# Summing the last expert layer into the output with TensorE instead of VectorE

## The chip, the cores and the metric

The kernel runs on one core of one Trainium2 chip. The metric is device time in microseconds (us), the median of several runs. A core has five engines, each with an instruction queue of its own: TensorE (PE; its weight loads are shown apart as PEld), VectorE (DVE), ScalarE (ACT), GpSimd (POOL) and SyncE (SP). SP, ACT and POOL also issue DMA transfers. The engines wait for each other through semaphores. PE reads two operands from SBUF, a stationary one that is loaded as weights and a moving one that is streamed, and writes into PSUM, where a row of matmuls can add up.

## The reference, cut to what matters

The program is four layers over an image tensor of 2 x 256 x 32 x 32. Only its last lines bear on the change: the residual sum of the mixture-of-experts layer, and the way back from tokens to an image.

```python
    logits = jnp.einsum('bsd,de->bse', x, gate_w) + gate_b
    probs = jax.nn.softmax(logits, axis=-1)
    top_probs, top_idx = jax.lax.top_k(probs, 2)
    top_probs = top_probs / jnp.sum(top_probs, axis=-1, keepdims=True)
    ...
    return jnp.einsum('bseo,bse->bso', expert_out, dispatch)
...
    t = t + _L3_ffn_ref(_ln_t(t), L3_ffn_gate_w, L3_ffn_gate_b, L3_ffn_w1, L3_ffn_w2, L3_ffn_w3)
    x = _from_tokens(t, x)      # t.transpose(0, 2, 1), then to 2 x 256 x 32 x 32
```

So for each of 2048 tokens, the output is t plus w0 times the row of its first expert plus w1 times the row of its second expert, and channels, not tokens, come first in the output.

## The kernel before, in words

Tokens lie 128 to a tile: t is an SBUF tensor of 128 x 16 x 256 (`NT` = 16 tiles of 256 channels, `C`). Four tiles (`TPC`) make a chunk of 512 tokens (`TC`); two chunks make an image (`NB` = 2). Channels are two halves of 128 (`NCC`, index cc).

`experts` runs the chosen experts group by group, 128 rows each. Its last step in a group is a copy on DVE (L1576) and an indirect DMA from POOL (L1577), which scatters the 128 result rows into a DRAM tensor `yd` of 4096 x 256: the first experts' rows of all tokens first, then the second experts' rows. How many groups run depends on the data; the last of them stand in nested branches (L1604).

The final stage begins at L1656, after the last branch. For each chunk, `combine` (L1364) loads the expert rows from `yd` with DMAs issued alternately by SP (k = 0) and ACT (k = 1), 24 in all, of one tile (128 KB) or two tiles (256 KB). Then DVE adds each row tile, times its weight column, into t (L1378): two sums to a tile, 32 in all. After that `net.transposed` (L175) turns the four tiles of the chunk on PE, half by half of the channels, into one PSUM bank of 128 x 512 (L179), and ACT copies the bank to the output tile (L1671) in the order of pixels that the image has. After the second chunk of an image, SP stores the two halves of the image (L1675), 512 KB each.

The order on each engine is that of the program: DVE's sums in order of tiles, PE's turnings behind them, ACT's copies behind those, and the row loads of ACT in the same queue as its copies. `make_identity` gives `net.ident`, the 128 x 128 identity in SBUF. `gates[1].weight` is 128 x 2 x 16: a column for each expert choice k and tile.

Of the kernel before, what the change touches and what calls it, by code (L numbers as in the profile page):

```python
# [10 lines left out]
F32 = mybir.dt.float32  # L11
# [5 lines left out]
PSUM = bass.MemoryType.PSUM  # L17
DRAM = bass.MemoryType.DRAM

P = 128  # L20
NB = 2
HW = 1024
W = 32
T = NB * HW
C = 256
NCC = C // P
NT = T // P
TC = 512
NCH = T // TC
TPC = TC // P  # L30
# [1333 lines left out]
def combine(net, gate, t, j, pool, n=TPC):  # L1364

    nc, layer = net.nc, gate.layer
    y = pool.tile([P, 2, TPC, C], F32, tag="yl", name=f"{layer}_yl_{j}")
    for i in range(0, TPC, n):
        for k, eng in enumerate((nc.sync, nc.scalar)):
            at = k * T + j * TC + i * P  # L1370
            eng.dma_start(
                y[:, k, i : i + n],
                gate.yd[at : at + n * P, :].rearrange("(i p) c -> p i c", p=P),
            )
    for i in range(TPC):
        ti = j * TPC + i
        for k in range(2):
            nc.vector.scalar_tensor_tensor(  # L1378
                t[:, ti, :], y[:, k, i, :], gate.weight[:, k, ti : ti + 1], t[:, ti, :],
                ALU.mult, ALU.add,  # L1380
            )
        if i % n == n - 1:
            yield
# [228 lines left out]
@with_exitstack  # L1612
def conv_attn_hybrid(ctx: ExitStack, tc: tile.TileContext, a: dict, out: bass.AP):
    nc = tc.nc
    net = Net(ctx, tc, a["cols"], a["rows"])
    main = ctx.enter_context(tc.tile_pool(name="main", bufs=1))
    x = main.tile([P, NCC, NB, HW], F32, name="x")
    lg = Taps.logits(main.tile([P, 40 * W], F32, tag="lg", name="lg0"))
    conv_dram = ctx.enter_context(tc.tile_pool(name="conv_dram", bufs=1, space=DRAM))
    with tc.tile_pool(name="conv_w", bufs=2) as convw:  # L1620
        def load_x(b):
            for cc in range(NCC):
                nc.sync.dma_start(x[:, cc, b, :], a["x"][b, cc])

        load_x(0)
        taps = Taps(net, convw, main, x, a["l1_w1"], a["l1_w2"])
        layer0(
            net, x, a["x"],
            [a[f"m1_{k}"] for k in ("in_w", "out_w", "xproj_w", "dt_w")],
            [a[f"m2_{k}"] for k in ("in_w", "out_w", "xproj_w", "dt_w")],  # L1630
            lambda: load_x(1), taps, conv_dram, lg,
        )
    tokens = ctx.enter_context(tc.tile_pool(name="tokens", bufs=1))
    t = tokens.tile([P, NT, C], F32, name="t")
    with (
        tc.tile_pool(name="counters", bufs=1) as counters,
        tc.tile_pool(name="gate", bufs=2) as gpool,
        tc.tile_pool(name="gate_dram", bufs=1, space=DRAM) as gdram,
    ):
        with ExitStack() as first:  # L1640
            weigh = layer1(first, net, x, t, taps, lg)
            net.counters(counters)
            gates = [Gate(net, n, t, a[f"{n}_gate_w"], gpool, gdram) for n in ("l2", "l3")]
            linear_attention(
                net, t, weigh, gates[0].chunk,
                *[a[f"l2_{k}"] for k in ("wq", "wkv", "wm", "w1", "w2")]
            )
        with tc.tile_pool(name="scores", bufs=1) as spool:
            scores = Scores(net, spool, a["l3_wqkv"])
            experts(net, "l2", gates[0], a["l2_experts"], scores.make)  # L1650
            softmax_attention(
                net, t, lambda *a: combine(net, gates[0], t, *a), gates[1].chunk,
                scores,
            )
        experts(net, "l3", gates[1], a["l3_experts"])
        with (  # L1656
            tc.tile_pool(name="f_sb", bufs=2) as sb,
            tc.tile_pool(name="f_y", bufs=4) as ypool,
            tc.tile_pool(name="f_ps", bufs=4, space=PSUM) as ps_f,
        ):  # L1660

            for b in range(NB):
                o = [sb.tile([P, HW], F32, tag=f"o{cc}", name=f"out_{b}_{cc}") for cc in range(NCC)]
                for a in range(2):
                    for _ in combine(net, gates[1], t, 2 * b + a, ypool, 1 if b == a else 2):
                        pass
                    for cc in range(NCC):
                        tiles = [t[:, (2 * b + a) * TPC + i, :] for i in range(TPC)]
                        ps = net.transposed(ps_f, tiles, cc, "mm")
                        to = o[cc].rearrange("p (r a h c) -> p a r c h", a=2, h=W // 2, c=2)  # L1670
                        nc.scalar.copy(  # L1671
                            to[:, a], ps.rearrange("p (r c h) -> p r c h", c=2, h=W // 2)
                        )
                        if a:
                            nc.sync.dma_start(out[b, cc], o[cc])  # L1675

# [73 lines left out]
```

## Time and profile before

| what | value |
|---|---|
| median of 3 runs | 2173.26 us (2171.8 to 2174.47) |
| the profiled execution's own time | 2172.59 us |
| its span, first to last instruction | 2170.9 us |
| granted PE clock over the span | 0.913 of full speed |
| PE busy over the span | 1889.3 us (87%) |
| DVE busy over the span | 1402.7 us (65%) |
| last scatter of expert rows landed | at 2146.80 us |
| DVE's 32 sums (L1378) of the final stage | from 2150.04 to 2164.5 us |
| ACT's last copy (L1671) ends | at 2166.15 us |

Times within the span count from its start. A row of the timeline or of the chain of waits begins with its start and its length in us; then come the engine, the line of the kernel, the operation, the tiles it writes and reads, and a count if rows were merged. In square brackets stands how long the engine had been idle before it and on what it waited. "x4: 272/278/2010" in an answer on one line gives the shortest, the median and the longest of four instructions in ns. Lines of matmuls overlap, since PE is pipelined.

### The profile page before, as it was taken

The page shows a single profiled execution, that of the slowest core. Times are in us where ns is not written, and L with a number is a line of the kernel's source. Part 1 is how long each engine was busy: PE and PEld are TensorE (multiplying, and loading weights), DVE is VectorE, ACT ScalarE, POOL GpSimd, SP SyncE. Part 2 cuts the span into 40 slices and gives each one's busy share as a digit, 9 for nine tenths or more (in the row PEclk, how much of TensorE's full clock was granted, in tenths as well). Part 3 has the DMA queues.
Part 4 walks back from the last instruction along what each step waited for, and adds up shares of the span by engine and source line. Part 5 has one row for each costly group of instructions (what it writes and reads, how often), then busy time and mean ns, then how long its engine had stood idle before and what let it go on. Part 6 is the DMA issues. An engine that isn't in the chain of part 4 may idle for free.

```text
span 2170.9 us, 27318 instructions
## 1 busy us (share of the span) xinstructions
PE 1889.3 (87%) x9652; PEld 1345.8 (62%) x9652; DVE 1402.7 (65%) x2210; ACT 959.9 (44%) x1611; POOL 1027.6 (47%) x726
## 2 busy tenths in 40 slices
PE   6888798888989879799989989949999699859996
PEld 2364555556555645455656556539999467649995
DVE  6999997999999999897405575652222544442223
ACT  4676776767777767653213454411010132301111
POOL 3796887959698695964225420012332000023331
PEclk8969988897989889899999999969999799979997
DMA  2121121111212111310030100028999200059998
GB/s 107 45 69 40 40 67 35 53 40 45 63 48 60 35 48 34 86 40 20 5 64 1 49 15 10 20 86 304 323 332 333 83 10 10 20 208 320 334 330 294
DMA packets 90499, 223.87 MB, mean 103 GB/s; under 512 B 35467, under 2 KB 51728, under 8 KB 79732
## 3 DMA queue, kind: packets, MB, share of 16 engines
q1 hardware_dynamic: 77636, 198.29, 27.2%
q0 software_dynamic: 7728, 19.15, 3.0%
q10 hardware_dynamic: 4992, 4.59, 0.7%
q8 instruction: 81, 1.33, 0.3%
q14 instruction: 62, 0.51, 0.1%
HBM read 204.60 MB, written 19.37 MB: 103 GB/s over the span
## 4 chain that ended last, share of the span: by engine, by line
PE 32%; DVE 22%; issue 19%; POOL 12%; ACT 9%; DMA 5%; POOLq 0%; SPq 0%; ACTq 0%; DVEq 0%
DVE m_h L472 11%; DVE m_ya L449 5%; PE acc L769 3%; POOL x L1527 3%; POOL l_yd L1577 3%; PE m_ht L440 3%; PE av L1283 3%; POOL m_h L461 3%; PE early_acc L769 2%; PE sc L1257 2%; ACT m_da L468 2%; DMA l_yd<-y,target 2%; PE h L1106 2%; PE w L1115 1%; PE m_xd_ps L351 1%
## 5 line engine op out<-in xcount | busy, mean ns | idle before, releaser
L461 POOL TENSOR_TENSOR m_h<-m_du,m_b 128x1024 f32<-128x1024 f32 x254 | 594.4, 2364 | 227.6 <-PE m_ht L440 126.8
L440 PE MATMUL m_ht<-ident,m_h 128*128 128x128 f32 x2048 | 360.2, 306 | 107.2 <-DVE m_ya L449 78.4
L440 PEld LDWEIGHTS m_ht<-ident,m_h 128*128 128x128 f32 x2048 | 266.2, 156 | 299.0 <-issue 105.2
L468 ACT ACTIVATE m_da<-m_delta,m_aneg 128x512 f32<-128x512 f32 x512 | 349.0, 690 | 219.7 <-DVE m_h L472 218.8
L1527 POOL DMA_INDIRECT x<-l_zd,source x82 | 84.5, 1031 | 569.9 <-DVE source L1472 215.3
L449 DVE SCALAR_TENSOR_TENSOR m_ya<-m_ht,m_ct,m_ya 128x512 f32<-128x512 f32 x448 | 319.3, 732 | 29.2 <-PE m_ht L440 27.8
L472 DVE TENSOR_TENSOR_SCAN m_h<-m_da,m_state,m_h 128x512 f32<-128x512 f32 x256 | 316.8, 1268 | 26.9 <-POOL m_h L461 20.7
L472 DVE TENSOR_TENSOR_SCAN m_h<-m_da,m_h 128x512 f32<-128x512 f32 x256 | 302.8, 1208 | 25.3 <-ACT m_da L468 15.2
L1557 PEld LDWEIGHTS h<-xts,we 128*128 128x128 f32 x2528 | 298.3, 194 | 6.8 <-issue 2.9
L1557 PE MATMUL h<-xts,we 128*128 128x128 f32 x2528 | 299.4, 277 | 1.9 <-issue 1.5
L1564 DVE TENSOR_TENSOR hid<-hid,h 128x512 f32<-128x512 f32 x79 | 54.3, 687 | 255.5 <-PE h L1557 252.0
L1563 ACT ACTIVATE hid<-h 128x512 f32<-128x512 f32 x79 | 47.2, 597 | 381.7 <-issue 299.3
L1571 PE MATMUL o<-we,hid 128*128 128x256 f32 x632 | 150.4, 380 | 2.2 <-DVE y L1576 1.6
L1577 POOL DMA_INDIRECT l_yd<-y,target x79 | 79.0, 1000 | 142.7 <-DVE y L1576 136.4
L1571 PEld LDWEIGHTS o<-we,hid 128*128 128x128 f32 x632 | 113.7, 190 | 15.7 <-DVE y L1576 2.8
L336 PE MATMUL m_conv<-m_pre,m_taps 128*128 128x512 f32 x240 | 114.6, 596 | 6.8 <-ACT m_gate L498 5.6
L769 PE MATMUL early_acc<-x,early 128*98 128x448 f32 (+24 forms) x308 | 100.5, 453 | 0.0
L769 PE MATMUL acc<-x,pair 128*98 128x416 f32 (+21 forms) x308 | 94.0, 452 | 0.0
L1576 DVE COPY y<-o 128x256 f32<-128x256 f32 x79 | 33.6, 425 | 69.3 <-PE o L1571 69.3
L309 PE MATMUL m_in<-x,m_in_sb 128*128 128x512 f32 x128 | 67.7, 653 | 7.6 <-ACT m_pre L313 5.2
L769 PEld LDWEIGHTS acc<-x,pair 128*98 128x98 f32 x308 | 47.6, 167 | 39.1 <-issue 33.6
L494 PE MATMUL m_g<-x,m_gate_sb 128*128 128x512 f32 x128 | 66.5, 633 | 3.9 <-ACT m_o L168 2.1
(318 smaller groups left out, 2849.2 us busy)
## 6 DMA issues: line engine op xcount, KB each, us to landing
we<-in_l_experts_dram SPq DMA_DIRECT2D x82, 1536.0 KB
m_b<-m_bd SPq DMA_DIRECT2D x128, 256.0 KB
w<-in_l_w_dram SPq DMA_DIRECT2D x21, 256.0 KB
l_zd<-l_z SPq DMA_DIRECT2D x7, 512.0 KB
l_yl<-l_yd SPq DMA_DIRECT2D x10, 256.0 KB
l_yl<-l_yd ACTq DMA_DIRECT2D x10, 256.0 KB
early<-taps SPq DMA_DIRECT2D x7, 343.0 KB
pair<-taps SPq DMA_DIRECT2D x7, 343.0 KB
```

The costliest lines, as they stand in the source:

```text
L309: nc.tensor.matmul(ps, lhsT=self.in_sb[:, kc, mc * P : (mc + 1) * P], rhs=self.xt[:, kc, tok], start=(kc == 0), stop=(kc == NCC - 1),)
L336: nc.tensor.matmul(ps, lhsT=self.taps[:, dc * 4 + k, :], rhs=pre[:, dc, k : k + TC], start=(k == 0), stop=(k == 3),)
L440: nc.tensor.transpose(ps[:, dc * P : (dc + 1) * P], hs[dc // G][:, dc % G, i * P : (i + 1) * P], net.ident,)
L449: nc.vector.scalar_tensor_tensor(ya[:, i, :], ps, c, ya[:, i, :], ALU.mult, ALU.add)
L461: (nc.vector if start and n == 0 else nc.gpsimd).tensor_mul(h, du[:, g * G : (g + 1) * G, :], b.unsqueeze(1).to_broadcast(half))
L468: nc.scalar.activation(da, delta[:, dc, :], AF.Exp, scale=self.aneg[:, i : i + 1])
L472: nc.vector.tensor_tensor_scan(h, da, h, 0.0 if first else state[:, n, dc : dc + 1], ALU.mult, ALU.add)
L769: nc.tensor.matmul(a[:, lo - 16 * k : hi - 16 * k, co : co + n], lhsT=lhsT, rhs=self.x[:, kc, b, lo - r0 : hi - r0, ci : ci + n], start=(u ...
L1527: nc.gpsimd.indirect_dma_start(out=x, out_offset=None, in_=zd[:, :], in_offset=bass.IndirectOffsetOnAxis(ap=source[:, g : g + 1], axis=0), ...
L1557: nc.tensor.matmul(ps[:, at], lhsT=w12[:, s, kc, at], rhs=xt[:, kc * P : (kc + 1) * P], start=(kc == 0), stop=(kc == NCC - 1),)
L1571: nc.tensor.matmul(ps[:, :C], lhsT=ht[:, mc * P : (mc + 1) * P], rhs=w[:, 8 + mc, :], start=(mc == 0), stop=(mc == NHC - 1),)
L1577: nc.gpsimd.indirect_dma_start(out=yd[g], out_offset=bass.IndirectOffsetOnAxis(ap=target[:, g : g + 1], axis=0), in_=y, in_offset=None, bo ...
```

## The change

DVE no longer sums and PE no longer turns finished sums. Instead PE does both at once: a matmul with a tile of t (or of expert rows) as the stationary operand and a 128 x 128 diagonal matrix as the moving one gives the turned tile, scaled token by token, and PSUM adds up the three terms: t with the identity, the first expert's rows with a diagonal of its weights, the second's with another. There are eight sums of 128 x 512, one to each PSUM bank.

- DVE makes the 32 diagonals `by` first, the identity times a weight column (L1668 of the new kernel).
- The rows are loaded by 16 DMAs of 256 KB, eight from SP and eight from ACT, all issued at the start of the stage, each into a tile of its own (L1675).
- POOL makes `wide`, 128 x 512: zero, with the identity in its first 128 columns. The first matmul into a bank uses it as its moving operand, and so writes all 512 columns.
- PE first turns all of t: 8 matmuls of 512 columns and 24 of 128, then for each chunk the 16 matmuls with expert rows, 64 in all (L1689).
- The eight copies from PSUM to the output tiles are made by DVE, six of them, and by ACT, the two of the second image's second half of channels (L1711, L1713). The four stores stay with SP.

In the built program the first instruction of this stage on each of the five engines waits for all that came before the last branch, the last scatter's landing included; before, DVE's, PE's and ACT's did so only through the loads. Nothing ahead of the stage moves on any engine.

```diff
-            tc.tile_pool(name="f_y", bufs=4) as ypool,
-            tc.tile_pool(name="f_ps", bufs=4, space=PSUM) as ps_f,
+            tc.tile_pool(name="f_y", bufs=1) as ypool,
+            tc.tile_pool(name="f_ps", bufs=1, space=PSUM) as ps_f,
         ):
+            by = ypool.tile([P, 2, NT, P], F32, name="f_by")
+            y = {}
+            ps = {}
+            for i in range(NT):
+                for k in range(2):
+                    nc.vector.tensor_scalar_mul(
+                        by[:, k, i, :], net.ident, gates[1].weight[:, k, i : i + 1]
+                    )
+            for i in range(0, NT, 2):
+                for k, eng in enumerate((nc.sync, nc.scalar)):
+                    at = k * T + i * P
+                    y[i, k] = ypool.tile([P, 2, C], F32, name=f"f_yl_{i}_{k}")
+                    eng.dma_start(
+                        y[i, k], gates[1].yd[at : at + 2 * P, :].rearrange("(i p) c -> p i c", p=P),
+                    )
+            wide = ypool.tile([P, TC], F32, name="f_wide")
+            nc.gpsimd.memset(wide, 0.0)
+            nc.gpsimd.tensor_copy(wide[:, :P], net.ident)
+
+            def turn(i, a, rhs, stop=False):
+                first = rhs is wide
+                at = i % TPC * P
+                for cc in range(NCC):
+                    to = ps[i // TPC, cc]
+                    nc.tensor.matmul(
+                        to if first else to[:, at : at + P], lhsT=a[:, cc * P : (cc + 1) * P],
+                        rhs=rhs, start=first, stop=stop,
+                    )
+
+            for i in range(NT):
+                if i % TPC == 0:
+                    for cc in range(NCC):
+                        ps[i // TPC, cc] = ps_f.tile([P, TC], F32, name=f"f_{i // TPC}_{cc}")
+                turn(i, t[:, i, :], net.ident if i % TPC else wide)
             for b in range(NB):
...
                 for a in range(2):
-                    for _ in combine(net, gates[1], t, 2 * b + a, ypool, 1 if b == a else 2):
-                        pass
+                    j = 2 * b + a
+                    for i in range(j * TPC, (j + 1) * TPC):
+                        for k in range(2):
+                            turn(i, y[i // 2 * 2, k][:, i % 2, :], by[:, k, i, :], stop=(k == 1 and i % TPC == TPC - 1))
                     for cc in range(NCC):
-                        tiles = [t[:, (2 * b + a) * TPC + i, :] for i in range(TPC)]
-                        ps = net.transposed(ps_f, tiles, cc, "mm")
-                        to = o[cc].rearrange("p (r a h c) -> p a r c h", a=2, h=W // 2, c=2)
-                        nc.scalar.copy(
-                            to[:, a], ps.rearrange("p (r c h) -> p r c h", c=2, h=W // 2)
-                        )
+                        to = o[cc].rearrange("p (r a h c) -> p a r c h", a=2, h=W // 2, c=2)[:, a]
+                        of = ps[j, cc].rearrange("p (r c h) -> p r c h", c=2, h=W // 2)
+                        if b and cc:
+                            nc.scalar.copy(to, of)
+                        else:
+                            nc.vector.tensor_copy(to, of)
                         if a:
                             nc.sync.dma_start(out[b, cc], o[cc])
```

## The prediction

> **What bounds the kernel now.** The diff touches only what follows the last expert, so I looked for where those last 30 us go. First the busy times by stretch of the end. Columns: stretch, its length, then busy us and (instructions) of PE, PE weight loads, DVE, ACT, POOL; last the granted PE clock, DMA share and GB/s.
>
> ```profile
> 2140.50:2147.00 6.50, 1.90 (x8) 1.34 (x8) 0.43 (x1) 0.00 (x0) 1.97 (x2) 0.93 0.30 107
> 2147.00:2150.00 3.00, 0.00 (x0) 0.00 (x0) 0.00 (x0) 0.00 (x0) 0.00 (x0) 0.50 0.59 170
> 2150.00:2155.00 5.00, 1.77 (x6) 0.90 (x6) 3.80 (x9) 0.00 (x0) 0.00 (x0) 0.50 0.96 303
> 2155.00:2160.00 5.00, 3.86 (x12) 1.83 (x12) 4.90 (x14) 1.65 (x4) 0.00 (x0) 0.50 1.09 350
> 2160.00:2164.00 4.00, 3.03 (x13) 1.79 (x12) 3.98 (x11) 1.59 (x3) 0.00 (x0) 0.50 0.98 369
> 2164.00:2166.00 2.00, 1.04 (x4) 0.29 (x2) 0.48 (x1) 0.93 (x2) 0.00 (x0) 0.50 0.01 4
> ```
>
> Between 2150 and 2164 DVE is full (12.7 of 14 us), but DMA is full too. VectorE is not the only limit: 4.19 MB of rows and the first image's 1.05 MB go out in that time at about 350 GB/s. PE is at half clock throughout. Then the chain of waits and the timeline say what begins and ends it:
>
> ```profile
> 2140.62 6.18 DMA l_yd<-y,target
> 2147.41 2.44 DMA l_yl<-l_yd
> 2164.01 0.50 DVE t L1378
> 2164.55 0.49 PE mm_t L179
> 2165.07 0.59 ACT out L1671
> ```
>
> The last scatter lands at 2146.80, the first rows at 2149.85; DVE's last sum ends at 2164.5. From ACT's first copy ending (2165.65) it is 0.8 us to the first byte of the last two outputs, 2.6 us of transfer and 1.8 us to the span's end at 2170.9. That tail stays.
>
> **The change, part by part.** All sums are against the profiled execution: span 2170.9, its time 2172.59; the median of the runs is 2173.26, so the difference is added to that.
>
> *Removed*: 32 sums on DVE (0.477 us each, one every 0.40 us, 12.7 us on the path), 32 turnings on PE that follow them one by one, eight copies on ACT (0.62 each, behind which ACT's last row load stood until 2158.97).
>
> *Start.* Before, each queue's first row load waited for the last scatter; now all five engines' first instruction of the part waits for everything before the branch, the scatter included. So DVE's diagonals and POOL's `wide` also begin only after 2146.80. About 11 wait instructions stand ahead of each; ACT's eight took 2146.84 to 2147.37, so I put DVE's first diagonal at 2147.55, POOL's memset at 2147.5, the loads some 0.2 us later than now.
>
> *DVE*: 32 products of 128x128 by a column. The same shape stands in the trace (one of four, and its neighbours):
>
> ```profile
> 1258.81 0.27 DVE L1034 TENSOR_TENSOR kvd<-kv,head 128x128 f32<-128x128 f32 x1
> 1259.01 0.27 DVE L1035 TENSOR_SCALAR ksd<-head,ks 128x128 f32<-128x128 f32 x1
> 1259.20 0.41 DVE L160 BATCH_NORM_STATS2 ln_st<-t 128x6 f32<-128x256 f32 x1
> ```
>
> 0.27 long, one start every 0.195: 32 take 6.2 us and end at 2153.8. The first row sum on PE comes later than that (below), so their cost is nothing as long as PE's turning of t covers them; without that cover the wait would be for one pair of diagonals at a time.
>
> *POOL*: memset of 128x512 (rows of 128x384 at 0.42 and 128x686 at 0.67 give 0.52), a copy of 128x128 (0.30 in the row of L863). Both meet DVE's run on shared SBUF ports; I add 0.13 each, for the reason given under the first rival. 2147.5 + 0.65 + 0.05 + 0.43 gives 2148.65, and PE starts at 2148.75.
>
> *PE* becomes the bound: everything it has stands in order behind the first matmul with `wide`. Prices from the first expert of this layer, cold and then warm:
>
> ```profile
> 1927.50:1931.00 3.50, 3.50 (x17) 3.50 (x18) 0.00 (x0) 0.00 (x0) 1.02 (x2) 0.50 1.10 297
> 1931.00:1933.00 2.00, 2.00 (x19) 1.99 (x18) 0.00 (x0) 1.51 (x2) 0.00 (x0) 0.97 0.78 250
> 1936.50 3.73 PE L1557 MATMUL h<-xts,we 128*128 128x128 f32 x32
> ```
>
> Warm: (3.73 - 0.28) / 31 = 0.111 us for each 128-column matmul. 512 columns: two scores matmuls (L1257) took 1.02 together, which is 0.43 each and 0.17 for the pipeline. Cold: 0.215 and 0.86 (L1229: four in 3.48). The turning of t is 8 wide and 24 narrow: 12.0 us cold, 6.1 warm. The 64 row matmuls: 13.8 cold, 7.1 warm. All warm 13.2.
>
> How long is it cold? The Trainium skill, "TensorE: Matmul & The Clock Gate", Part 1: half rate after an idle window of about 3.4 us, full rate after a busy one, the windows free-running. The trace agrees: matmuls ended at 2142.4 and the clock fell at 2146.1; they ran densely from 1927.45 and it rose at 1931.1 (3.65 us). So PE begins cold and warms after 3.4 to 6.8 us, by the window's phase; I take 5. Each cold us does half a us of work: 13.2 + 5/2 = 15.7, plus 0.17 for the last one's pipeline. PE ends at 2164.6 (now 2165.24).
>
> *Loads*: sixteen of 256 KB in place of 24; at 350 GB/s from 2148.4 the last bytes are in at 2160.4 and usable about 2161.2. By then PE is just half through: t ends near 2157.4 (5 us cold do 5/12.0, the rest takes 3.6), and the row matmuls of the eighth pair are due at 2163.7. So the loads are hidden, with 2.5 us to spare.
>
> *Copies*: the last two now run side by side, DVE (128x512 from PSUM: 0.69 in the row of L1280) and ACT (0.62): 2164.7 to 2165.4. Now ACT's first ends at 2165.65. DVE's five earlier copies fall between 2159 and 2164 in its idle time, and the first image's outputs go out about 2162.5 to 2165.5, when loads are over: cover free, price 2.6 us if they met the last outputs.
>
> *Tail*: 2165.4 + 0.8 + 2.6 + 1.75 = 2170.55, against 2170.9: **0.35 us less, 2172.9**. VectorE's 12.7 us leave the path, and PE's 15.7, begun 1.3 us earlier than DVE's, take their place.
>
> **The rivals.**
>
> *POOL is starved (ends slower).* The Trainium skill, "SBUF — State Buffer", Who interferes with whom: a DVE instruction in a two-port mode and a GpSimd one exclude each other, whichever came first, for its length; and "VectorE: DVE Perf Modes", Mode 2×_2P: fp32 tensor_scalar from SBUF enters it. The trace agrees in that one of the four L1035 took 2.01 us beside a POOL sum. DVE's 32 diagonals stand without a gap. If POOL gets in only at the end of such a run, `wide` is ready at 2153.8 + 0.52 + 0.35, PE starts at 2154.7, ends at 2170.6, the span at 2176.5: 5.6 more, **2178.9**. It decides 0.2% (4.3 us) when PE starts after 2153.4. For it: a POOL copy of 12 columns (0.20 otherwise) once waited through five DVE sums. Against it: POOL beside four column products of DVE, back to back.
>
> ```profile
> 48.75 4.04 POOL L305 COPY m_pre<-m_carry 128x12 f32<-128x12 f32 x1 [25.69 <-DVE m_du L405]
> 1170.76 2.64 POOL L906 TENSOR_SCALAR band<-diag,half 32x112 f32<-32x112 f32 x4 [2.00 <-PE bt L920]
> 1170.89 1.42 DVE L173 TENSOR_SCALAR z<-t,ln_mv,ln_rs 128x256 f32<-128x256 f32 x4
> ```
>
> There POOL's took 0.66 to 0.70 where 0.553 is usual: it lost about 0.13 each and was not held for the run. That is the kind of instruction the change uses, so I take this and keep the other end for the range.
>
> *The loads decide.* If PE starts or warms early enough, rows usable at 2161.2 set the end: eight matmuls and the last pipeline (1.1), copy (0.75), then 5.15 of tail give 2168.2, 2.7 less, **2170.5**. Against it: the first image's 1.05 MB would then be sent among the loads, giving back up to 2.6.
>
> *PE stays cold.* Now it is at half clock with PE busy 77% of a stretch. Then 12.0 + 13.8 + 0.2 from 2148.75 ends at 2174.75, the span at 2180.6: **2183**. Against: a matmul stream without gaps, as at 1927.45, was warm after one window, and t's turning waits for nothing after its first instruction.
>
> That VectorE's work is removed for nothing in return is excluded: diagonals and matmuls do stand in the built order. A gain beyond 4.3 us would need loads faster than the 350 GB/s shown.
>
> **How the numbers follow.** Likeliest 0.65, its own range 2171.3 to 2174.8 (warming at 3.4 or 6.8 us is 0.85 each way, the start 0.5, the tail 0.5). Loads decide 0.13. POOL starved 0.14. Cold 0.04. PE late by something not shown, such as its longer instruction stream, 0.04. About 0.2% of this kernel's time is what a measurement can tell from no change. Faster than that: 0.03, from the loads case. Slower: 0.12 of the starved case, the cold and the late one, 0.20. Same: 0.77. The range from 2170.4 to 2179.0 leaves out the cold case and the worse half of the others.
>
> **What would show it.** Right: PE's first L1689 at about 2148.7, clock rising between 2152 and 2156, DVE's diagonals ending near 2154, PE's last at 2164 to 2165 without waiting for rows, a last copy 0.7 after it. Wrong: POOL's memset or copy lasting several us (starved); PE waiting for `f_yl` at its end (loads); a clock of 0.50 to the end; or outputs overlapping the loads.

## The result, and the profile after

| | kernel before | changed kernel |
|---|---|---|
| median of 5 runs | 2174.47 us (2171.8 to 2181.6) | 2187.66 us (2184.08 to 2190.35) |
| profiled execution, and its span | 2172.59, 2170.9 us | 2187.32, 2185.6 us |
| PE busy, records | 1889.3 us, 9652 | 1910.8 us, 9812 |

The changed kernel takes 1.0054 of the time before (95% interval 1.0038 to 1.0070), which is 11.7 us more; the medians lie 13.2 us apart. The forecast was 2172.9, with a range from 2170.4 to 2179.0; the result lies above it.

What lies ahead of the final stage shifts by several us from one execution to the next, in any kernel. The last scatter's issue (L1577) came at 2143.14 in the profile before and at 2145.45 in the one after, and as late as 2152.80 in the profiles of the experiments. So from here on the *stage* is measured from the issue of the last scatter to the end of the span: 2170.9 - 2143.14 = **27.8 us before**, 2185.6 - 2145.45 = **40.2 us after**. The 12.4 us between them are the loss; the forecast's stage was 2170.55 - 2143.14 = 27.4.

First the stretches of the changed kernel's end, with the columns of the prediction's table (length, then busy us and instructions of PE, PE weight loads, DVE, ACT and POOL, the PE clock, DMA share, GB/s):

```profile
2149.50:2151.30 1.80, 0.00 (x0) 0.00 (x0) 0.53 (x3) 0.00 (x0) 0.81 (x2) 0.50 0.13 29
2151.30:2155.00 3.70, 3.66 (x6) 1.63 (x7) 3.70 (x20) 0.00 (x0) 0.00 (x0) 0.52 0.99 310
2155.00:2165.00 10.00, 10.00 (x58) 7.13 (x57) 2.24 (x12) 0.00 (x0) 0.00 (x0) 1.00 0.94 301
2165.00:2180.00 15.00, 14.85 (x133) 14.65 (x132) 3.61 (x6) 0.75 (x2) 0.00 (x0) 1.00 0.18 71
```

PE is full from 2151.34 to 2179.86, and nothing else is full all that time: DVE is done with its diagonals at 2157.2, and DMA has little to do after 2165. The mean clock of 0.52 in the second stretch says that it rises from 0.50 to 1.00 at about 2154.85, 3.5 us after PE's start; half speed for so long costs less than 2 us. So neither a wait nor the clock explains why PE needs so much longer than forecast. The chain of waits says it in one line:

```profile
2150.41 0.52 POOL f_wide L1681
...
2151.34 28.52 PE f L1689 x192
...
2179.88 0.61 ACT out L1711
```

28.52 us of PE without a gap, and a count of 192. The program has 8 + 24 + 64 = 96 matmuls at L1689. The groups of the stage, each with its count, busy us, mean ns of one, and idle us before them:

```profile
L1689 PE MATMUL f<-f_by,f_yl 128*128 128x128 f32 x128 | 14.5, 275 | 0.0
L1689 PEld LDWEIGHTS f<-f_by,f_yl 128*128 128x128 f32 x128 | 14.4, 192 | 0.0
L1689 PE MATMUL f<-f_wide,t 128*128 128x512 f32 x16 | 9.3, 715 | 6.6 <-POOL f_wide L1682 6.6
L1689 PE MATMUL f<-ident,t 128*128 128x128 f32 x48 | 6.0, 275 | 0.0
L1713 DVE COPY out<-f 128x512 f32<-128x512 f32 x6 | 4.0, 689 | 19.1 <-PE f L1689 19.1
```

Each count is twice the program's: 128 records for 64 matmuls with rows, 16 for 8, 48 for 24. The whole kernel gained 9812 - 9652 = 160 PE records, which is 192 added less the 32 turnings taken away (the turnings, transposes, have one record each). So one fp32 matmul of this program runs as two records on PE, each with a weight load of its own; from here on one such record is called a pass. The profile before showed it already, in these two groups of its page:

```profile
L1557 PE MATMUL h<-xts,we 128*128 128x128 f32 x2528 | 299.4, 277 | 1.9 <-issue 1.5
L1564 DVE TENSOR_TENSOR hid<-hid,h 128x512 f32<-128x512 f32 x79 | 54.3, 687 | 255.5 <-PE h L1557 252.0
```

L1564 runs once for each group of 128 rows, so there were 79 groups, and 2528 / 79 = 32 records for each. The loops around L1557 make 2 x 4 x 2 = 16 matmuls. The prediction quoted a row with "x32" and took it for 32 matmuls.

### The profile page after: what moved, and what is told of

Read it like the earlier page. It is cut to its first block, busy times and chain, and to the rows that moved or that the text cites. A ratio compares the mean times of both kernels' runs of the same rounds, so it can differ in the third digit from the quotient of the medians.

```text
span 2185.6 us, 27670 instructions
## 1 busy us (share of the span) xinstructions
PE 1910.8 (87%) x9812; PEld 1365.5 (62%) x9812; DVE 1400.6 (64%) x2216; ACT 956.6 (44%) x1605; POOL 1028.0 (47%) x728
## 4 chain that ended last, share of the span: by engine, by line
PE 42%; DVE 20%; issue 13%; ACT 10%; POOL 10%; DMA 4%; POOLq 0%; SPq 0%; DVEq 0%; ACTq 0%
DVE m_h L472 11%; PE h L1557 6%; DVE m_ya L449 5%; PE acc L769 3%; POOL m_h L461 3%; PE o L1571 3%; PE m_ht L440 3%; PE av L1283 3%; PE sc L1257 2%; ACT m_da L468 2%; PE h L1106 2%; PE early_acc L769 2%; DMA l_yd<-y,target 2%; POOL x L1527 2%; POOL l_yd L1577 2%
## 5 line engine op out<-in xcount | busy, mean ns | idle before, releaser
L1557 PEld LDWEIGHTS h<-xts,we 128*128 128x128 f32 x2528 | 296.7, 193 | 6.3 <-issue 2.5
L1557 PE MATMUL h<-xts,we 128*128 128x128 f32 x2528 | 297.6, 276 | 1.7 <-issue 1.5
L1564 DVE TENSOR_TENSOR hid<-hid,h 128x512 f32<-128x512 f32 x79 | 54.3, 687 | 256.7 <-PE h L1557 253.1
L1577 POOL DMA_INDIRECT l_yd<-y,target x79 | 79.0, 1000 | 142.6 <-DVE y L1576 136.3
```

The source lines that it names most:

```text
L1557: nc.tensor.matmul(ps[:, at], lhsT=w12[:, s, kc, at], rhs=xt[:, kc * P : (kc + 1) * P], start=(kc == 0), stop=(kc == NCC - 1),)
L1577: nc.gpsimd.indirect_dma_start(out=yd[g], out_offset=bass.IndirectOffsetOnAxis(ap=target[:, g : g + 1], axis=0), in_=y, in_offset=None, bo ...
```

## The experiments

The theory after the result: **what failed is the count of passes**; each fp32 matmul of 128 columns costs PE two of them, 0.11 us each at full clock, and the loss is those extra passes. Rivals: the new loads, the late start of PE behind POOL's `wide`, the hand-overs of the new stage, and another reason for slow passes (the columns streamed, the weights loaded). In summary, with the kernel before and after first:

| run | stage, us | ratio to before (95%) |
|---|---|---|
| before | 27.8 | |
| after | 40.2 | 1.0054 (1.0038 to 1.0070) |
| one pass (bf16 halves) | 26.0 | 0.9984 (0.9976 to 0.9993) |
| half the streamed columns | 40.9 | 1.0053 (1.0035 to 1.0071) |
| t turned by transposes | 30.9 | 0.9991 (0.9982 to 1.0000) |
| loads alone | 27.2 | 0.9986 (0.9976 to 0.9996) |
| one expert by DVE, one by PE | 28.0 | 0.9997 (0.9988 to 1.0006) |
| half the weight columns | 41.4 | 1.0062 (1.0044 to 1.0081) |
| half of both | 35.4 | 1.0040 (1.0024 to 1.0056) |
| `wide` made early | 35.9 | 1.0037 (1.0022 to 1.0053) |
| tiles shared | 27.7 | 1.0001 (0.9990 to 1.0013) |
| rows in one pass, `wide` early | 26.8 | 0.9990 (0.9974 to 1.0006) |

The stage is that of one profiled execution, the ratio that of all timed ones.

### One pass for each matmul

Every matmul of the stage reads only the upper halves (bf16) of its fp32 operands. The same matmuls, loads, diagonals and copies remain; what is left out is the lower half of the bits of t, of the rows and of the weights.

```diff
+                high = lambda v: v.bitcast(BF16).rearrange("p (c h) -> p c h", h=2)[:, :, 1]
...
-                        to if first else to[:, at : at + P], lhsT=a[:, cc * P : (cc + 1) * P],
-                        rhs=rhs, start=first, stop=stop,
+                        to if first else to[:, at : at + P], lhsT=high(a[:, cc * P : (cc + 1) * P]),
+                        rhs=high(rhs), start=first, stop=stop,
```

> The changed kernel, with all 96 matmuls of the last stage reading only the upper halves of their fp32 numbers, as bf16 (the lower halves are left out of the sums); every instruction, load and wait stays. Theory: an fp32 matmul is two passes over its columns, each with a weight load of its own, and PE is the bound with 192 passes. With one pass each PE's 28.5 us fall to about 15.5, 13 us less: 2174 to 2176 us, near the kernel before. Rival, what the prediction priced (one pass already; the time is lost elsewhere, at the start of the stage or in a wait): no change, about 2187.

Measured: ratio 0.9984, stage 26.0 us, 14.2 less than the changed kernel. From its timeline (start, length, then in brackets what PE waited for):

```profile
2157.88 0.58 PE L1690 MATMUL f<-f_wide,t 128*128 128x512 bf16 x1 [6.52 <-POOL f_wide L1682]
...
2162.84 1.19 PE L1690 MATMUL f<-f_by,f_yl 128*128 128x128 bf16 x18
...
2170.27 1.94 PE L1690 MATMUL f<-f_by,f_yl 128*128 128x128 bf16 x14 [0.32 <-DMA f_yl<-l_yd]
```

PE starts as late as before behind `wide` (2157.88 - 2152.11 = 5.8 us after the last scatter's issue), has all that the change gave it, and yet the loss is gone. The row matmuls have 64 records for 64, and towards the end they wait for the loads. So with less work on PE the prediction's rival "the loads decide" is what happens, and PE's fp32 work is the cause of the loss. This run doesn't separate the number of passes from the price of one: 18 bf16 passes took 1.19 us, about 0.055 each when the 0.2 us of the last one's pipeline is taken off, half of an fp32 pass. The number is shown by the counts above: 192 passes at the prices per record that the prediction used make 26.4 us, and the start at half clock makes the rest. What the price of a pass consists of is the question of the next three runs.

### Half the columns streamed

The matmuls with rows stream 64 of the 128 columns of their diagonal, so half of the tokens of each tile get no expert rows.

```diff
-            def turn(i, a, rhs, stop=False):
+            def turn(i, a, rhs, stop=False, n=P):
...
-                        to if first else to[:, at : at + P], lhsT=a[:, cc * P : (cc + 1) * P],
-                        rhs=rhs, start=first, stop=stop,
+                        to if first else to[:, at : at + n], lhsT=a[:, cc * P : (cc + 1) * P],
+                        rhs=rhs if first else rhs[:, :n], start=first, stop=stop,
...
-                            turn(i, y[i // 2 * 2, k][:, i % 2, :], by[:, k, i, :], stop=(k == 1 and i % TPC == TPC - 1))
+                            turn(i, y[i // 2 * 2, k][:, i % 2, :], by[:, k, i, :], stop=(k == 1 and i % TPC == TPC - 1), n=P // 2)
```

> The changed kernel, with the 64 row matmuls streaming 64 columns in place of 128 (half of each tile's tokens get no expert rows). Weight loads stay. If the streaming of columns sets PE's pace, each of the 128 passes falls from 0.112 to about 0.056 us: 7 us less, about 2180. If the loading of weights sets it (128 columns each, unchanged): no change, about 2187.

Its row matmuls and their weight loads, from the timeline:

```profile
2166.72 14.37 PEld L1689 LDWEIGHTS f<-f_by,f_yl 128*128 128x128 f32 x128
2166.83 14.40 PE L1689 MATMUL f<-f_by,f_yl 128*128 128x64 f32 x128
```

14.40 us, where the changed kernel's took 14.46. The theory that streaming alone sets the pace of a pass fell.

### Half the weights, and half of both

For 56 of the 64 row matmuls only 64 weight columns are loaded, so half of the channels get no expert rows from them; and once more with the 64 streamed columns too.

```diff
-                        to if first else to[:, at : at + P], lhsT=a[:, cc * P : (cc + 1) * P],
-                        rhs=rhs, start=first, stop=stop,
+                        to if first else to[:m, at : at + n], lhsT=a[:, cc * P : cc * P + m],
+                        rhs=rhs if first else rhs[:, :n], start=first, stop=stop,
...
-                            turn(i, y[i // 2 * 2, k][:, i % 2, :], by[:, k, i, :], stop=(k == 1 and i % TPC == TPC - 1))
+                            turn(i, y[i // 2 * 2, k][:, i % 2, :], by[:, k, i, :], *((True, P) if k == 1 and i % TPC == TPC - 1 else (False, P // 2)), P)
```

The last line is that of half the weights, where n stays P; the run with half of both ends it with `P // 2`.

> 56 of the 64 matmuls with expert rows use 64 columns of weights in place of 128 (half of the channels get no expert rows from these tiles), streaming 128 columns as in the changed kernel. Theory 'the weight load alone sets the pace of a pass, and takes as long as its columns': row phase 16 x 0.112 + 112 x 0.06 = 8.5 us instead of 14.46, ratio to the kernel before 1.0025. Theory 'load and stream each need the 0.112': row phase stays at 14.4, ratio 1.005. Theory 'a load costs the same for any number of columns': 14.4 too, and then the next run, with both halved, stays there as well.

> As the run with half the weights, and 64 streamed columns too in all 64 (about a quarter of the work with expert rows is done). Theory 'load and stream each need the 0.112, and each goes with its columns': 16 x 0.112 + 112 x 0.056 = 8.1 us for the row phase instead of 14.46, ratio to the kernel before 1.0025. Theory 'a fixed cost of a load': 14.4, ratio 1.005.

The row matmuls of the first, and then of the second:

```profile
2168.03 15.44 PE L1689 MATMUL f<-f_by,f_yl 128*64 128x128 f32 x128
```

```profile
2164.14 9.52 PE L1689 MATMUL f<-f_by,f_yl 128*64 128x64 f32 x128
```

Halving the load alone saves nothing (15.44, even 1 us more, which stays unexplained); halving both saves 4.9 us. So an fp32 pass of 128 x 128 is held at 0.112 us from both sides: with the load or the stream halved, the other still keeps the pace. The second came out longer than the 8.1 us expected: its narrow passes took about 0.066 us instead of 0.056 (7.4 us in 112 of them). The theory that load and stream each need the 0.112 us held; that each shrinks in proportion to its columns did not hold exactly, and why is not shown. The Trainium skill, "TensorE: Matmul & The Clock Gate", Part 2, Back-to-back issue gap, says that the spacing is set by both operations; these three runs agree.

### t turned by transposes

t is turned by 32 transposes, one record each, in place of the 32 matmuls. The row matmuls then write over it, so t is left out of the sum.

```diff
-                        rhs=rhs, start=first, stop=stop,
+                        rhs=rhs, start=not stop, stop=stop,
...
-                turn(i, t[:, i, :], net.ident if i % TPC else wide)
+                for cc in range(NCC):
+                    nc.tensor.transpose(
+                        ps[i // TPC, cc][:, i % TPC * P : (i % TPC + 1) * P],
+                        t[:, i, cc * P : (cc + 1) * P], net.ident,
+                    )
...
-                            turn(i, y[i // 2 * 2, k][:, i % 2, :], by[:, k, i, :], stop=(k == 1 and i % TPC == TPC - 1))
+                            turn(i, y[i // 2 * 2, k][:, i % 2, :], by[:, k, i, :], stop=(k == 1))
```

> The changed kernel, with t turned by 32 transposes of 128 columns, in place of 8 wide and 24 narrow matmuls (the row matmuls then write over them, so t is left out of the sum). Theory of passes: a transpose of fp32 is one pass, so t's 12.2 us warm become 3.6; with what is cold, 7 to 9 us less, about 2179. Rival (passes cost the same for both, or t's turning is hidden behind loads and costs nothing): 2185 to 2187.

Measured: ratio 0.9991, stage 30.9 us, 9.3 less than the changed kernel and more than expected. PE's timeline:

```profile
2149.16 5.35 PE L1699 MATMUL f<-ident,t 128*128 128x128 f32 x32 [2.76 <-PEq L1604]
2155.23 0.68 PE L1689 MATMUL f<-f_by,f_yl 128*128 128x128 f32 x4 [0.71 <-DMA f_yl<-l_yd]
2156.28 2.02 PE L1689 MATMUL f<-f_by,f_yl 128*128 128x128 f32 x16 [0.37 <-DVE f_by L1668]
2160.00 12.30 PE L1689 MATMUL f<-f_by,f_yl 128*128 128x128 f32 x108 [1.70 <-DMA f_yl<-l_yd]
```

Two things came together. t takes 5.35 us, 3.4 of them at half clock, in place of the 14.05 of the changed kernel (2151.34 to 2165.39): that is 8.7 us. And PE begins 2.0 us after the last scatter's issue instead of 5.9, since nothing waits for `wide`: 3.9 us more. Of the 12.6, 2.8 are lost again in waits for rows and diagonals, and 0.5 in the row matmuls, which come in three runs instead of one. This run mixes two causes, so the start was tried alone.

### `wide` made early

The changed kernel, with POOL's memset and copy moved ahead of the third layer's scores.

```diff
+        wide = wpool.tile([P, TC], F32, name="f_wide")
+        nc.gpsimd.memset(wide, 0.0)
+        nc.gpsimd.tensor_copy(wide[:, :P], net.ident)
         with tc.tile_pool(name="scores", bufs=1) as spool:
...
-            wide = ypool.tile([P, TC], F32, name="f_wide")
-            nc.gpsimd.memset(wide, 0.0)
-            nc.gpsimd.tensor_copy(wide[:, :P], net.ident)
```

> The changed kernel with POOL's wide made before the third layer's scores instead of in the final stage. Theory 'PE's start is set by wide, then 28.5 us of passes': PE begins 2.0 us after the last scatter's issue instead of 5.9, the pass count is unchanged, and the stage takes 36.3 us instead of 40.15: ratio to the kernel before 1.0037. Theory 'the start is covered by something else (rows or diagonals decide)': PE waits later, and less than 1.5 us is won: ratio 1.005.

```profile
2145.30 2.67 PE L1690 MATMUL f<-f_wide,t 128*128 128x512 f32 x4 [2.41 <-PEq L1604]
2147.78 2.48 PE L1690 MATMUL f<-ident,t 128*128 128x128 f32 x12
```

PE begins 1.7 us after the last scatter's issue (2143.63), works for 28.42 us, and the stage is 35.9: 4.3 less than the changed kernel, where 36.3 was expected. PE's own time is unchanged, and the earlier start (by 4.2 us) comes through in full, so PE alone sets the end. It also shows that PE's first matmul does not wait for the scatter to land: the row loads, which need the landed rows, were issued only at 2147.96, and DVE's first diagonal came at 2148.72.

### The loads alone

The kernel before, with nothing but the 16 loads of 256 KB up front.

```diff
+            for i in range(0, NT, 2):
+                for k, eng in enumerate((nc.sync, nc.scalar)):
...
+                    eng.dma_start(
+                        y[i, k], gates[1].yd[at : at + 2 * P, :].rearrange("(i p) c -> p i c", p=P),
+                    )
...
-                    for _ in combine(net, gates[1], t, 2 * b + a, ypool, 1 if b == a else 2):
-                        pass
+                    for i in range(j * TPC, (j + 1) * TPC):
+                        for k in range(2):
+                            nc.vector.scalar_tensor_tensor(
+                                t[:, i, :], y[i // 2 * 2, k][:, i % 2, :],
+                                gates[1].weight[:, k, i : i + 1], t[:, i, :], ALU.mult, ALU.add,
+                            )
```

> The kernel before, with the changed kernel's sixteen loads of 256 KB at the start of the stage and nothing else of the change. Theory: loads are not the cause; VectorE's 32 sums still set the end, and the short idle stretch of DMA at 2150 goes: 0 to 1.5 us less than before, 2172.5 to 2174.5. Rival (the first rows come later in larger pieces, or the stage's first waits are the loss): 2 to 10 us more than before.

Measured: ratio 0.9986 (0.9976 to 0.9996), stage 27.2. The loads are no part of the loss; by themselves they help a little. DVE's sums then run with one short wait, and take 13.3 us from first to last where they took 14.5 before:

```profile
2160.30 3.25 DVE L1676 SCALAR_TENSOR_TENSOR t<-f_yl,l_weight,t 128x256 f32<-128x256 f32 x8 [7.78 <-DMA f_yl<-l_yd]
...
2163.87 9.70 DVE L1676 SCALAR_TENSOR_TENSOR t<-f_yl,l_weight,t 128x256 f32<-128x256 f32 x24 [0.32 <-DMA f_yl<-l_yd]
```

This version is faster than both kernels, by about 0.14% against the kernel before.

### Sharing the work between DVE and PE

Two attempts at a better version in fp32. Neither uses `wide`. In the first, DVE adds the first experts' rows, and PE turns the t so summed (by transposes) and adds the second experts' rows; DVE and ACT make four copies each:

```diff
+                        nc.vector.scalar_tensor_tensor(
+                            t[:, i, :], y[i // 2 * 2, 0][:, i % 2, :],
+                            gates[1].weight[:, 0, i : i + 1], t[:, i, :], ALU.mult, ALU.add,
+                        )
...
+                            nc.tensor.matmul(
+                                ps[j, cc][:, at], lhsT=t[:, i, cc * P : (cc + 1) * P], rhs=net.ident,
+                                start=True, stop=False, is_transpose=True,
+                            )
...
-                        for k in range(2):
-                            turn(i, y[i // 2 * 2, k][:, i % 2, :], by[:, k, i, :], stop=(k == 1 and i % TPC == TPC - 1))
+                            nc.tensor.matmul(
+                                ps[j, cc][:, at], lhsT=y[i // 2 * 2, 1][:, i % 2, cc * P : (cc + 1) * P],
+                                rhs=by[:, i, :], start=False, stop=True,
+                            )
```

> DVE adds the first experts' rows into t (16 sums of about 0.48 us), PE turns the finished sums (32 single records) and adds the second experts' rows by 32 matmuls (64 records) with 16 diagonals; all 16 loads up front. Theory 'two passes on a full PE': PE has 32 x 0.06 + 64 x 0.112 = 9 us of warm work instead of 26.4 and is no longer the bound; the loads (about 18 us from the last scatter's issue to the last row) and 7 us behind them are, so the stage takes 25.2 to 26.5 us against 27.8 before: ratio to before 0.998 to 0.9995. Theory 'something else about the new stage costs (diagonals, waits, DVE's copies)': DVE now has 16 sums, 16 diagonals and copies, more than PE, and the stage stays above 30: ratio over 1.001.

Measured: no difference (0.9997), stage 28.0, where 25.2 to 26.5 was expected. Two stretches of it:

```profile
2156.90:2161.00 4.10, 3.74 (x16) 3.40 (x17) 2.03 (x6) 0.00 (x0) 0.00 (x0) 0.50 1.02 340
...
2163.00:2170.00 7.00, 7.00 (x64) 6.88 (x63) 5.39 (x12) 1.57 (x3) 0.00 (x0) 1.00 0.61 205
```

PE is full again. A tile (two turnings and four passes) starts every 0.665 us at full clock, so a turning costs 0.11 us like a pass, and not the 0.06 that the expectation took; 16 tiles are 10.6 us, and 4 us at half clock cost 2 more. PE, which begins at 2156.95, 8.9 us after the last scatter's issue, and ends at 2170.1, sets the end here, and not the loads.

In the second, DVE sums the even tiles whole, and PE the odd ones; ACT makes seven of the eight copies:

```diff
+                        for k in range(2):
+                            nc.vector.scalar_tensor_tensor(
+                                t[:, even, :], y[even, k][:, 0, :],
+                                gates[1].weight[:, k, even : even + 1], t[:, even, :], ALU.mult, ALU.add,
+                            )
+                        for i in (even + 1, even):
...
+                                    ps[j, cc][:, at], lhsT=t[:, i, cc * P : (cc + 1) * P], rhs=net.ident,
+                                    start=True, stop=i == even, is_transpose=True,
...
+                            for k in range(2 * (i - even)):
```

> Of each pair of tiles DVE sums one (two sums of 0.48 us) and PE turns it finished; the other is turned and summed by PE alone with diagonals (2 + 8 records). All 16 loads up front, nearly all copies by ACT, all in fp32. Theory 'passes of 0.11 us against loads': per pair PE has 4 single records and 8 of two-pass matmuls, 12 x 0.11 = 1.3 us, DVE 1.0 us, the loads 1.5 us; the loads decide but for 1 to 2 us that the slow clock costs at the start: stage 26.3 to 27.3 us from the last scatter's issue (before 27.8), ratio to the kernel before 0.9985 to 0.9997. Theory 'the handing over between DVE and PE costs, as in the version with the experts shared': stage 28 or more, ratio 1.000 or over.

Measured: no difference (1.0001), stage 27.7, between the 26.3 to 27.3 of the one theory and the 28 of the other. PE's first matmul with rows began at 2158.22, 9.2 us after the last scatter's issue, and its last instruction ended at 2170.8. Two stretches that cover this time:

```profile
2158.20:2162.50 4.30, 4.28 (x18) 4.06 (x19) 2.77 (x9) 0.00 (x0) 0.00 (x0) 0.50 1.06 354
2162.50:2170.80 8.30, 8.28 (x72) 7.85 (x70) 4.46 (x12) 3.44 (x6) 0.00 (x0) 1.00 1.04 355
```

PE is full in both, so it sets the end here too, and not a wait in the handing over. The 4.3 us at half clock cost about 2.1 us of full speed, a little more than the 1 to 2 us allowed for.

### Rows in one pass, t in two

The changed kernel with `wide` early, and only the rows and their diagonals read as bf16 upper halves (the lower halves of the rows and of the weights are left out; t keeps its fp32).

```diff
+            def high(v):
+                return v.bitcast(BF16).rearrange("p (c h) -> p c h", h=2)[:, :, 1]
...
-                        to if first else to[:, at : at + P], lhsT=a[:, cc * P : (cc + 1) * P],
-                        rhs=rhs, start=first, stop=stop,
+                        to if first else to[:, at : at + P], lhsT=part(a[:, cc * P : (cc + 1) * P]),
+                        rhs=part(rhs), start=first, stop=stop,
...
-                            turn(i, y[i // 2 * 2, k][:, i % 2, :], by[:, k, i, :], stop=(k == 1 and i % TPC == TPC - 1))
+                            turn(i, y[i // 2 * 2, k][:, i % 2, :], by[:, k, i, :], stop=(k == 1 and i % TPC == TPC - 1), part=high)
```

For t, `part` leaves its operand as it is.

> The changed kernel with wide made early and only the rows and diagonals read as bf16 (their upper halves; t is still turned in fp32). PE: t 13.9 us from 1.7 us after the last scatter's issue, so to 15.6; then 64 records of rows at 0.06 = 3.7 us, but the last rows are usable only at 18.2 and set the end. Theory 'passes are what the change costs, then the loads decide': stage 25.5 to 26.5 us (before 27.8, the changed kernel 40.15), ratio to the kernel before 0.998 to 0.999. Theory 'PE's start and t's turning cost by themselves': stage over 28, ratio over 1.000.

```profile
2145.93 1.95 PE L1693 MATMUL f<-f_wide,t 128*128 128x512 f32 x4 [2.35 <-PEq L1604]
...
2158.23 2.11 PE L1693 MATMUL f<-f_by,f_yl 128*128 128x128 bf16 x34
...
2163.62 1.21 PE L1693 MATMUL f<-f_by,f_yl 128*128 128x128 bf16 x14 [0.80 <-DMA f_yl<-l_yd]
```

Stage 26.8 us, 0.3 above the range expected and 13.4 below the changed kernel's; against the kernel before the interval reaches over 1, so whether it is faster stays open. Here the clock was still up when PE began, and stayed up: t took 2158.23 - 2145.93 = 12.3 us. The prediction had 6.1 for that. And 34 single bf16 records took 2.11 us, 0.057 each when the 0.2 of the last one's pipeline is taken off; two fp32 passes are 0.224, 3.9 times that. Towards the end PE waits for rows, as the last line shows.

## Why the prediction was wrong, by its own steps

- **Start: nearly right in time, in part by luck and wrong in its reason.** PE at 5.6 us after the last scatter's issue was predicted, 5.9 measured, and two errors partly cancelled: from the landing to POOL's memset it took 1.1 us and not 0.7, and from the memset to PE's start 0.9 us and not 1.25. And PE itself does not wait for the landing, as the prediction and the section on the change say of all five engines; it waited for `wide` alone, as the run with `wide` early shows.
- **DVE's diagonals: right.** 6.47 us (6.2 predicted), ended at 2157.2, and the first matmul with rows came at 2165.39. They cost nothing.
- **POOL: right, and the rival "starved" fell, though the memset hardly tested it.** POOL's memset (0.52 us) had run for 0.36 us when DVE's first diagonal began. The copy stood wholly beside the diagonals. The prediction took from the Trainium skill ("SBUF — State Buffer", Who interferes with whom) that one of the two blocks the other for the length of an instruction; the traces agree that one of them loses time, about 0.12 us and not a whole run of diagonals. In the changed kernel the copy took 0.29 us, as usual, and the diagonal beside it 0.391 us in place of 0.273; in the one-pass run the copy took 0.40 us, and no diagonal more than 0.31. So the 0.13 us that the prediction added to the copy had about the right size, but it can fall on either engine. The changed kernel's two groups, then the one-pass run's two (shortest, median and longest of one in ns):

```profile
L1668 DVE TENSOR_SCALAR f_by<-ident,l_weight x32: 271/273/391, 2150.8 to 2157.0; 128x128 f32<-128x128 f32 x32
L1682 POOL COPY f_wide<-ident x1: 287/287/287, 2151.0 to 2151.0; 128x128 f32<-128x128 f32 x1
```

```profile
L1668 DVE TENSOR_SCALAR f_by<-ident,l_weight x32: 270/272/310, 2157.2 to 2163.3; 128x128 f32<-128x128 f32 x32
L1682 POOL COPY f_wide<-ident x1: 400/400/400, 2157.4 to 2157.4; 128x128 f32<-128x128 f32 x1
```

- **PE: the step that failed.** "Warm: (3.73 - 0.28) / 31 = 0.111 us for each 128-column matmul" is right for a record: the changed kernel's rows took (14.46 - 0.28) / 127 = 0.112. But it was multiplied by the 24 + 64 matmuls of 128 columns, and the program's fp32 matmuls are two records each. The 0.43 for 512 columns was half a matmul likewise. So the term "All warm 13.2" should have been twice that, 26.4 us: 12.2 for t (12.3 measured in the run whose clock was up all through) and 14.2 for the rows (14.46 measured). With 1.75 us for the cold start, the measured parts make the 28.52 us of PE, where 15.85 stood in the sum: 12.67 too little, and the forecast's stage of 27.4 missed the measured one by 12.7.
- **Clock: right.** It rose 3.5 us after PE's start (3.4 to 6.8 predicted, 5 taken); the rival "PE stays cold" fell. The cold part cost 1.75 us (t took 14.05 us, and 12.3 in the run whose clock was up), predicted 2.5.
- **Loads: right.** The last bytes were predicted 17.3 us after the last scatter's issue; DMA moved them until about 2163.7, 18.2 us after it, long before PE wanted them. The rival "the loads decide" is what the one-pass run became, with a stage of 26.0 us.
- **Copies and tail: right.** The last two copies ran side by side, 0.69 and 0.61 us, and from PE's end to the span's end it was 5.7 us (5.95 predicted).

The chances were spread over rivals that all counted one record for each matmul; even the worst of them, with PE cold to the end, came to 2183, short of the result. What would have found the error was one division: records of a group in the profile by matmuls of its loop. The Trainium skill counts in another way: "FP8 and Floating Point Precision", TensorE Precision Notes, has true fp32 at four passes through the array. The runs agree in time, with 3.9 bf16 passes for one fp32 matmul, while the records show two.

## What to carry to other kernels

Before a price per record is multiplied by a count of matmuls from the program, divide the records of a known group by the calls in its loop: here an fp32 matmul is two records and a transpose one. Work moved from VectorE to TensorE in fp32 pays that factor: the sums that looked like 13 us for PE were 26, more than the 13 us of DVE that they replaced. Issuing the loads early, alone, gave a small gain (0.14%) without any of it.

## What the runs showed of the hardware that was not expected

- An fp32 matmul of 128 x 128 x 128 is two records, each with its own weight load, 0.224 us together at full clock; with bf16 operands it is one of 0.057. An fp32 transpose is one record of about 0.11.
- In an fp32 pass, halving the streamed columns alone (14.40 us) or the weight columns alone (15.44) saved nothing of 14.46 us; halving both gave 9.52 (the weights were halved in 56 of the 64 matmuls).
- An early start does not keep PE's clock up for certain. In three runs PE had steady work from 1.6 to 2.0 us after the last scatter's issue on, and the clock was still up then. In the one with rows in one pass it stayed up (12.3 us for t). With `wide` early it fell at 2146.4, 1.1 us into the work, and was up again 3.4 us later; with t turned by transposes it fell 0.6 us into the work for 3.4 us. In the changed kernel, begun at 5.9 us, the clock had fallen before, and t took 14.05.
- The 32 transposes of 5.35 us brought PE's clock back up at 2153.15, before any other matmul of the stage; in the kernel before, the same 32 with gaps between them ran at half clock throughout.
- A POOL copy beside 32 DVE products in a row was not held for the run: either it or one product lost about 0.12 us.
